# Deformable attention on one core: the first image's softmax beside the second image's position network

## The chip, the core and the metric

The kernel runs on one core of a Trainium2 chip. Its engines are named as in the profile: PE (TensorE, matmuls and transposes; PEld is its weight load), DVE (VectorE), ACT (ScalarE), POOL (GpSimd) and SP (SyncE, which here only issues DMAs). Each engine takes its instructions in order; they meet through semaphores. The metric is the device time of one execution in microseconds, lower is better. The kernel before takes 3842.15 us, the median of three runs (3840.60 to 3842.97).

## What is computed

Four layers run one after the other on x of 2 images x 512 channels x 32 x 32, all in float32. The change touches layer 0, an attention of 1024 queries over 64 sampled keys with 8 heads per image. To each score comes a bias: a small network with two hidden layers of 128, computed for each pair of query and key from their difference in position. Cut to what matters:

```python
bias = jnp.sign(pos) * jnp.log1p(jnp.abs(pos))
bias = relu(bias @ cpb_w1 + cpb_b1)
bias = relu(bias @ cpb_w2 + cpb_b2)
bias = (bias @ cpb_w3 + cpb_b3).reshape(b, GROUPS, H * W, Hd * Wd)
sim = jnp.einsum('bhid,bhjd->bhij', qh, kh) + bias
attn = jax.nn.softmax(sim, axis=-1)
out = jnp.einsum('bhij,bhjd->bhid', attn, vh)
out = jnp.einsum('bchw,oc->bohw', out, out_w) + out_b
x = x + out                                  # then an MLP of 2048 hidden channels
```

Layers 1 to 3 (a deformable convolution with gathers, a linear attention, a full attention) follow.

## The kernel before, in words

**Tiling.** A tile has 128 partitions and usually 1024 columns, the pixels of an image. Two heads share a tile, 64 keys each, so that the scores of both images are eight tiles: `simT[:, p, :]` with p = 0 to 3 for image 0 and p = 4 to 7 for image 1.

**The position network** (`biased_scores`) is one loop over p and j, where j goes over the 32 pairs of keys of a half: 8 x 16 = 128 steps. A step handles eight keys in four groups (t = 0 to 3), each of two keys:

- `hidden` (L868): DVE adds the two parts of the first layer into a tile h (128x1024). A relu follows, on DVE (L875) for three keys of sixteen and on ACT (L877) for the others. There are six h buffers, so that DVE can be at most three groups ahead of PE.
- `second_layer` (L888): PE multiplies the pair of h by w2 into two tiles `ph` of two PSUM banks each, 8 matmuls for each, four at a time in different columns of the array. ACT drains the first (`lo`, L898) and the second (`hi`, L900), and DVE adds them, weighted (L901). The pool `ps_h` has three buffers of ph. They take turns: the third ph after one needs its buffer again.
- `last_layer` (L909): PE sums the four `hi` of the step before over the 128 hidden units into `sim`, two further PSUM banks. It is issued after the second group of a step.
- At step j = 0 DVE stores the finished scores of the p before (`store`, L931). At j = 8 and j = 24, `first_layer` loads the next parts (`ab`) through SP and scales four tiles on ACT (L533).

**The softmax** (`Softmax`). `attention(p)` transposes the scores of one p on PE, eight transposes into one tile `pt` (L992), so that the keys lie along the columns; DVE takes the maximum of each run of 64 (L998) and subtracts it into `e` (L1000); ACT takes exp in place (L1001); DVE sums (L1003), inverts (L1004) and multiplies (L1005). `turn(p, e)` transposes back on PE into `pb` (L1012), and ACT copies it over the scores in simT (L1017). For image 0 this stands at the end of `biased_scores`, in the PSUM buffers of the network (`pt` and `pb` are tiles of `ps_h`, with the same tag as `ph`) and in its SBUF buffers. Image 1's softmax is done later, woven into the MLP of image 0, through `Softmax.image`.

**What follows.** `projected` multiplies the values by the output weights (`pm`, L1040, copied by ACT at L1041), `project` multiplies the attention of image 0 by that (`po`, L1052), and the MLP of image 0 begins (`ph`, L1112; `acc`, L1101). Its second weights `mlp_w2` (4 MB) are loaded through SP (L217) when the network's buffers come free.

**What sets the order.** PE runs in the order in which the code calls it (a manual schedule). DVE and ACT are ordered by the framework's scheduler, which may put an instruction that is ready ahead of one that stands earlier in the code. Semaphores and buffers' waits come from the framework. A pool's buffer is given again when its last reader is done.

Of the kernel before, what the change touches and what calls it, by code (L numbers as in the profile page):

```python
# [10 lines left out]
F32 = mybir.dt.float32  # L11
# [7 lines left out]
CC = 4  # L19
HW = 1024  # L20
# [230 lines left out]
def chain(*parts):  # L251
    for part in parts:
        yield from part
# [23 lines left out]
def layers(net, out):  # L277
# [12 lines left out]
    with ExitStack() as later:  # L290
# [12 lines left out]
        with ExitStack() as l0a:  # L303
            l0a.enter_context(net.tc.manual_schedule(engines={mybir.EngineType.PE}))

            q_flat = new_room()[:, : (NP * 36 + 6) * 34]
            q_pad = q_flat[:, : NP * 36 * 34].rearrange("p (n y x) -> p n y x", y=36, x=34)
            keys = net.pool(l0a, "l0_k")
            kbd = keys.tile([128, NP, 128], F32, name="kbd", tag="kbd")
            dram = net.pool(l0a, "cpb_dram", space=bass.MemoryType.DRAM)  # L310
            feat = dram.tile([32, 2048], F32, name="feat_d", tag="feat_d")
            w2 = keys.tile([128, 128], F32, name="w2_t", tag="w2")
            first = net.pool(l0a, "cpb_ab", 4)
            parts = queries_keys_values(net, bn, simT, q_flat, q_pad, kbd, val, feat, first)
            nc.sync.dma_start(out=w2, in_=net.ins["w2"])

            def load_weights():
                t = new_room()
                w1 = t[:, : 4 * 2048].rearrange("p (k m) -> p k m", m=2048)
                out_w = t[:, 4 * 2048 :].rearrange("p (k m) -> p k m", m=C)  # L320
                nc.sync.dma_start(out=out_w, in_=net.ins["out_w"])
                nc.sync.dma_start(out=w1, in_=net.ins["mlp_w1"])
                return w1, out_w

            w1, out_w = biased_scores(
                net, q_pad, kbd, feat, w2, simT, first, parts, load_weights
            )
# [499 lines left out]
def biased_scores(net, q_pad, kbd, feat, w2, simT, first, parts, load_weights):  # L827
# [12 lines left out]
    with ExitStack() as ctx:  # L840
        small = net.pool(ctx, "cpb_w", 1)
        hid1 = net.pool(ctx, "cpb_h1", 6)
        lows = net.pool(ctx, "cpb_lo", 2)
        highs = net.pool(ctx, "cpb_hi", 6)
        ps_h = net.psum(ctx, "cpb_ps_h", 3)
# [6 lines left out]
        size = small.tile([128, 1], F32, name="size", tag="size")  # L852
# [51 lines left out]
        def last_layer(sim, j, sums):  # L904


            for n in range(2):
                for t in range(4):
                    nc.tensor.matmul(  # L909
                        sim[32 * t : 32 * t + 32, half(n)],  # L910
                        lhsT=w3[:, 30 - j : 62 - j],
                        rhs=sums[t][:, half(n)],
                        start=(j == 0),
                        stop=(j == 30),
                        skip_group_check=True,
                    )
# [13 lines left out]
        def store(p, sim):  # L930
            nc.vector.tensor_scalar(simT[:, p, :], sim, net.vec("cpb_b3"), None, ALU.add)  # L931

        pending = None
        sim = None
        hidden_done = 0
        for p, j in [(p, j) for p in range(NP) for j in range(0, 32, 2)]:
# [20 lines left out]
                if p == NP - 1:  # L957
                    weights = load_weights()
            pending = (p, j, sums)


        def two_banks(name):
            return ps_h.tile([128, HW], F32, name=name, tag="ph")

        def one(name, size):
            if size == HW:
                pool, tag = (hid1, "h1") if name == "e" else (highs, "hi")
                return pool.tile([128, HW], F32, name=name, tag=tag)
            return small.tile([128, size], F32, name=name, tag=f"soft_{name}", bufs=2)

        soft = Softmax(net, simT, one, two_banks)
        es = [soft.attention(p) for p in range(2)]
        last_layer(sim, *pending[1:])
        es += [soft.attention(p) for p in range(2, CC)]
        for p, e in enumerate(es):
            soft.turn(p, e)
        store(NP - 1, sim)
        return weights

# [1 line left out]
class Softmax:  # L981
# [4 lines left out]
        self.net, self.simT, self.one, self.banks = net, simT, one, banks  # L986

    def attention(self, p):
        nc, one = self.net.nc, self.one
        pt = self.banks("pt").rearrange("p (h j) -> p h j", j=64)  # L990
        for c in range(8):
            nc.tensor.transpose(  # L992
                pt[:, 2 * c : 2 * c + 2, :].rearrange("p h j -> p (h j)"),
                self.simT[:, p, 128 * c : 128 * c + 128],
                self.net.cst("ident"),
            )
        m = one("m", 16)
        nc.vector.tensor_reduce(m, pt, AX.X, ALU.max)  # L998
        e = one("e", HW).rearrange("p (h j) -> p h j", j=64)
        nc.vector.tensor_tensor(e, pt, m.unsqueeze(2).to_broadcast([128, 16, 64]), ALU.subtract)  # L1000
        nc.scalar.activation(e, e, AF.Exp)  # L1001
        s = one("s", 16)
        nc.vector.tensor_reduce(s, e, AX.X, ALU.add)  # L1003
        nc.vector.reciprocal(s, s)  # L1004
        nc.vector.tensor_tensor(e, e, s.unsqueeze(2).to_broadcast([128, 16, 64]), ALU.mult)  # L1005
        return e

    def turn(self, p, e):

# [1139 lines left out]
```

## Time and profile before

| | us |
|---|---|
| median of three runs (lowest, highest) | 3842.15 (3840.60, 3842.97) |
| the profiled execution | 3841.13 |
| its span, from the first to the last instruction | 3839.4 |
| mean granted TensorE clock | 0.990 |

By stretches of the span (a program sums each engine's busy time between two times):

| stretch, us | what runs | PE | DVE | ACT |
|---|---|---|---|---|
| 0 to 88 | queries, keys, values, sampling | 64.1 | 58.3 | 63.2 |
| 88 to 2104 | position network, both images | 2004.0 | 1914.7 | 1955.5 |
| 2104 to 2135 | softmax of image 0, start of the projection | 19.0 | 21.3 | 12.4 |
| 2135 to 2430 | projections, softmax of image 1, MLP of image 0 | 295.0 | 53.4 | 48.1 |
| 2430 to 3839 | MLP of image 1, layers 1 to 3 | 1352.6 | 717.4 | 487.6 |

The page gives busy times and, for the idle time of an engine, what ended it (the releaser). A row of the timeline has its start, its duration, engine, line, operation, what it writes and reads, how many instructions are merged into it (xN), and in brackets the idle time before it with its releaser. A float32 matmul shows as two records, one for each of its two passes. The duration of one instruction includes its start and its end, which lie beside the neighbours; in a row of work without gaps, an instruction costs the time from its start to the next one's start, which is less.

### The profile page before, as it was taken

The page shows a single profiled execution, that of the slowest core. Times are in us where ns is not written, and L with a number is a line of the kernel's source. Part 1 is how long each engine was busy: PE and PEld are TensorE (multiplying, and loading weights), DVE is VectorE, ACT ScalarE, POOL GpSimd, SP SyncE. Part 2 cuts the span into 40 slices and gives each one's busy share as a digit, 9 for nine tenths or more (in the row PEclk, how much of TensorE's full clock was granted, in tenths as well). Part 3 has the DMA queues.
Part 4 walks back from the last instruction along what each step waited for, and adds up shares of the span by engine and source line. Part 5 has one row for each costly group of instructions (what it writes and reads, how often), then busy time and mean ns, then how long its engine had stood idle before and what let it go on. Part 6 is the DMA issues. An engine that isn't in the chain of part 4 may idle for free. (4 is left out here: it accounts for less than half of the span.)

```text
span 3839.4 us, 59395 instructions
## 1 busy us (share of the span) xinstructions
PE 3734.6 (97%) x25356; PEld 1492.3 (39%) x25356; DVE 2765.1 (72%) x3242; ACT 2566.8 (67%) x2941; POOL 188.2 (5%) x180
## 2 busy tenths in 40 slices
PE   7999999999999999999999899999979999899999
PEld 4532222223222322232233444444434544455555
DVE  6999999999999999999999310510475482566565
ACT  7999999999999999999999211211123243345544
POOL 0000000000000000000000000000252150000000
PEclk9999999999999999999999999999989999999999
DMA  3000000000000000000010000022455471000000
GB/s 111 1 23 23 23 1 23 23 23 12 12 23 23 21 3 23 23 23 1 23 56 29 33 0 1 18 82 77 134 173 187 144 273 48 1 12 1 1 20 25
DMA packets 54459, 168.57 MB, mean 44 GB/s; under 512 B 4804, under 2 KB 10436, under 8 KB 51252
## 3 DMA queue, kind: packets, MB, share of 16 engines
q1 hardware_dynamic: 31556, 83.77, 6.3%
q0 software_dynamic: 21776, 79.14, 6.2%
q8 instruction: 200, 3.28, 0.4%
q10 hardware_dynamic: 864, 1.86, 0.1%
q14 instruction: 63, 0.52, 0.0%
HBM read 156.11 MB, written 8.65 MB: 43 GB/s over the span
## 5 line engine op out<-in xcount | busy, mean ns | idle before, releaser
L888 PE MATMUL ph<-h,w_t 128*32 128x512 f32 x16384 | 1796.8, 593 | 14.0 <-ACT lo L898 6.5
L868 DVE TENSOR_TENSOR h<-ab 128x1024 f32<-128x1024 f32 x1024 | 1206.0, 1219 | 73.2 <-PE ph L888 72.2
L888 PEld LDWEIGHTS ph<-h,w_t 128*32 128x32 f32 x16384 | 548.7, 110 | 1235.5 <-issue 1031.2
L877 ACT ACTIVATE h<-h 128x1024 f32<-128x1024 f32 x832 | 869.6, 1065 | 44.4 <-DVE h L868 40.6
L901 DVE SCALAR_TENSOR_TENSOR hi<-lo,low_w,hi 128x1024 f32<-128x1024 f32 x512 | 655.0, 1279 | 27.4 <-ACT hi L900 26.8
L900 ACT ACTIVATE hi<-ph,size_b,size 128x1024 f32<-128x1024 f32 x512 | 620.5, 1212 | 15.5 <-PE ph L888 10.1
L898 ACT ACTIVATE lo<-ph,vec_t 128x1024 f32<-128x1024 f32 x512 | 571.1, 1116 | 3.8 <-PE ph L888 3.8
L2071 ACT ACTIVATE e<-pl,m 128x1024 f32<-128x1024 f32 x128 | 143.6, 1122 | 228.1 <-DVE m L2063 228.1
L1552 PE MATMUL po<-fold,turned 128*128 128x512 f32 x576 | 269.7, 612 | 3.1 <-DVE dfacc L1560 2.9
L2063 DVE TENSOR_REDUCE m<-pl 128x1 f32<-128x1024 f32 x128 | 150.8, 1220 | 144.4 <-PE pl L1973 144.4
L1120 ACT ACTIVATE h<-ph,vec_t 128x512 f32<-128x512 f32 x64 | 44.0, 687 | 310.9 <-PE ph L1112 310.4
L909 PE MATMUL sim<-hi,w 128*32 128x512 f32 x2048 | 246.1, 592 | 0.6 <-DVE hi L901 0.6
L1112 PE MATMUL ph<-xn,room 128*128 128x512 f32 x512 | 230.2, 593 | 0.0
L1101 PE MATMUL acc<-h,mlp_w_t 128*128 128x512 f32 x512 | 229.8, 592 | 0.0
L1499 DVE SCALAR_TENSOR_TENSOR sum<-got,wts,sum 128x256 f32<-128x256 f32 x432 | 184.4, 479 | 48.1 <-ACT sum L1495 45.7
L1475 POOL DMA_INDIRECT got<-table,idx x144 | 174.0, 1209 | 550.4 <-DVE sum L1499 272.1
L2025 PE MATMUL pt<-cst_t,e 128*128 128x128 f32 x1024 | 148.2, 278 | 6.5 <-ACT aT L2036 3.9
L2025 PEld LDWEIGHTS pt<-cst_t,e 128*128 128x128 f32 x1024 | 117.9, 141 | 93.2 <-issue 61.0
L1552 PEld LDWEIGHTS po<-fold,turned 128*128 128x128 f32 x576 | 107.8, 197 | 114.8 <-issue 109.7
L1101 PEld LDWEIGHTS acc<-h,mlp_w_t 128*128 128x128 f32 x512 | 97.3, 190 | 122.5 <-issue 122.0
L1112 PEld LDWEIGHTS ph<-xn,room 128*128 128x128 f32 x512 | 96.2, 190 | 117.2 <-issue 116.6
L1526 ACT COPY turned<-pt 128x512 f32<-128x512 f32 x72 | 41.9, 582 | 145.9 <-PE pt L1520 145.7
(250 smaller groups left out, 2712.1 us busy)
## 6 DMA issues: line engine op xcount, KB each, us to landing
ab<-feat_d SPq DMA_DIRECT2D x64, 512.0 KB, 3.8
room<-in_dc_w_dram SPq DMA_DIRECT2D x9, 1024.0 KB, 4.7
dc_w_t<-in_dc_w_dram SPq DMA_DIRECT2D x5, 1024.0 KB, 4.8
room<-in_mlp_w_dram SPq DMA_DIRECT2D x1, 4096.0 KB
mlp_w_t<-in_mlp_w_dram SPq DMA_DIRECT2D x1, 4096.0 KB, 13.4
dc_w_t<-in_dc_w_dram SPq DMA_DIRECT2D x8, 512.0 KB, 5.1
w_qkv_t<-in_w_qkv_dram SPq DMA_DIRECT2D x3, 1024.0 KB, 8.9
out_dram<-x_all SPq DMA_DIRECT2D x12, 256.0 KB, 2.0
```

The source lines that it names most:

```text
L868: nc.vector.tensor_tensor(h1.rearrange("p (y x) -> p y x", x=32), at_x[:, k : k + 1, :].to_broadcast([128, 32, 32]), at_y[:, k, :].unsquee ...
L877: nc.scalar.activation(h1, h1, AF.Relu)
L888: nc.tensor.matmul(ph[32 * t : 32 * t + 32, half(n)], lhsT=w2[:, c0 : c0 + 32], rhs=pair[t // 2][:, half(n)], start=True, stop=True, skip_ ...
L898: nc.scalar.activation(lo, phs[0], AF.Relu, bias=b2_lo)
L900: nc.scalar.activation(hi, phs[1], AF.Relu, bias=size_b, scale=size)
L901: nc.vector.scalar_tensor_tensor(hi, lo, low_w, hi, ALU.mult, ALU.add)
L909: nc.tensor.matmul(sim[32 * t : 32 * t + 32, half(n)], lhsT=w3[:, 30 - j : 62 - j], rhs=sums[t][:, half(n)], start=(j == 0), stop=(j == 30 ...
L1101: nc.tensor.matmul(accs[oc], lhsT=self.w2[:, m, 128 * oc : 128 * oc + 128], rhs=hs[m], start=(m == 0), stop=(m == 15),)
L1112: nc.tensor.matmul(ph, lhsT=self.w1[:, k, 128 * m : 128 * m + 128], rhs=xn[:, k, :], start=(k == 0), stop=(k == CC - 1),)
L1499: nc.vector.scalar_tensor_tensor(t[:, q, :], g[:, s, :], w, t[:, q, :], ALU.mult, ALU.add)
L1552: nc.tensor.matmul(self.out, lhsT=turned[:, at : at + 128], rhs=self.folded.w[k][:, i, :], start=(k == 0 and i == 0), stop=(k == 8 and i = ...
L2025: nc.tensor.transpose(pt[:, 128 * c : 128 * c + 128], e[:, 128 * k : 128 * k + 128], ident)
```

## The change

The softmax of image 0 is cut into steps and moved into the loop of the position network, to where it works on image 1 (p from 4 to 7). `Softmax.attention` becomes a generator, `parts`, that yields after the subtraction, after the sum and after the multiplication; `steps` runs through them and then through `turn`. The loop takes one step at every fourth j (j = 4, 12, 20 and 28), sixteen steps in all for the four tiles of image 0. The small tiles and `e` get a pool of their own with one buffer of each (`cpb_e`), while `pt` and `pb` stay tiles of the ring of three `ph` buffers. `attention` runs through all parts as before, for image 1. Behind the loop only the last `last_layer` and `store` are left.

```diff
@@ biased_scores
+        exps = net.pool(ctx, "cpb_e", 1)
+
+        def two_banks(name):
+            return ps_h.tile([128, HW], F32, name=name, tag="ph")
+
+        def one(name, size):
+            return exps.tile([128, size], F32, name=name, tag=f"soft_{name}")
+
+        soft = Softmax(net, simT, one, two_banks)
+        beside = chain(*(soft.steps(p) for p in range(CC)))
+
         pending = None
         sim = None
         hidden_done = 0
...
             pending = (p, j, sums)
-
-
-        def two_banks(name):
-            return ps_h.tile([128, HW], F32, name=name, tag="ph")
-
-        def one(name, size):
-            if size == HW:
-                pool, tag = (hid1, "h1") if name == "e" else (highs, "hi")
-                return pool.tile([128, HW], F32, name=name, tag=tag)
-            return small.tile([128, size], F32, name=name, tag=f"soft_{name}", bufs=2)
-
-        soft = Softmax(net, simT, one, two_banks)
-        es = [soft.attention(p) for p in range(2)]
+            if p >= CC and j % 8 == 4:
+                next(beside, None)
+        for _ in beside:
+            pass
         last_layer(sim, *pending[1:])
-        es += [soft.attention(p) for p in range(2, CC)]
-        for p, e in enumerate(es):
-            soft.turn(p, e)
         store(NP - 1, sim)
         return weights

@@ class Softmax
     def attention(self, p):
+        parts = self.parts(p)
+        for e in parts:
+            pass
+        return e
+
+    def steps(self, p):
+        for e in self.parts(p):
+            yield
+        self.turn(p, e)
+        yield
+
+    def parts(self, p):
         nc, one = self.net.nc, self.one
...
         nc.vector.tensor_tensor(e, pt, m.unsqueeze(2).to_broadcast([128, 16, 64]), ALU.subtract)
+        yield e
         nc.scalar.activation(e, e, AF.Exp)
         s = one("s", 16)
         nc.vector.tensor_reduce(s, e, AX.X, ALU.add)
+        yield e
         nc.vector.reciprocal(s, s)
         nc.vector.tensor_tensor(e, e, s.unsqueeze(2).to_broadcast([128, 16, 64]), ALU.mult)
-        return e
+        yield e
```

## The prediction

> **What bounds the kernel now.** I read the page first, then the stage's busy time by windows, then the waits, then the timeline where the stage ends. The page's chain of waits is of no use here: its earliest piece lies at 2781 us, after everything that the change touches. The page's slices show where to look: between 88 and 2104 us (the position network of both images) all three big engines are nearly full, and just behind lies a hole. The windows, one over a whole pass p of 16 steps (247 us) and three over the end of the stage:
>
> ```profile
> core 0: us, PE busy (x) PEld busy (x) DVE busy (x) ACT busy (x) POOL busy (x), PEclk, DMA share, GB/s
> 1572.00:1819.00 247.00, 245.48 (x2272) 72.80 (x2264) 234.68 (x213) 240.80 (x236) 0.00 (x0) 1.00 0.06 18
> 2112.00:2120.00 8.00, 1.72 (x11) 1.55 (x12) 8.00 (x10) 3.12 (x3) 0.00 (x0) 0.76 0.41 174
> 2120.00:2128.00 8.00, 4.54 (x22) 3.80 (x21) 6.46 (x8) 2.98 (x3) 0.00 (x0) 0.50 0.00 0
> 2136.00:2164.00 28.00, 28.00 (x66) 12.19 (x65) 8.20 (x12) 0.41 (x1) 0.00 (x0) 1.00 0.00 0
> ```
>
> In a pass PE is idle for 1.5 of 247 us: it is the bound, one step each 15.45 us. DVE is idle for about 12 us and ACT for 6. From 2112 us it is the other way round: DVE is full, PE works little, and its granted clock falls to 0.76 and 0.50. The timeline of PE over that hole:
>
> ```profile
> 2104.05 1.97 PE L992 MATMUL pt<-cst_t,simT 128*128 128x128 f32 x16
> 2105.95 1.06 PE L909 MATMUL sim<-hi,w 128*32 128x512 f32 x6
> ...
> 2114.72 1.06 PE L1012 MATMUL pb<-cst_t,e 128*128 128x128 f32 x8 [3.27 <-DVE e L1005]
> 2119.34 1.94 PE L1012 MATMUL pb<-cst_t,e 128*128 128x128 f32 x8 [3.56 <-DVE e L1005]
> 2124.00 1.94 PE L1012 MATMUL pb<-cst_t,e 128*128 128x128 f32 x8 [2.72 <-DVE e L1005]
> 2126.68 1.94 PE L1012 MATMUL pb<-cst_t,e 128*128 128x128 f32 x8 [0.74 <-DVE e L1005]
> 2129.72 5.51 PE L1040 MATMUL pm<-room,val 128*128 128x512 f32 x8 [1.10 <-ACT simT L1017]
> 2135.06 1.45 PE L1052 MATMUL po<-simT,outv 128*128 128x512 f32 x3
> ```
>
> The last matmul of the network starts before 2104.05; the first of the next full stretch (L1052) at 2135.06. These **31.0 us** are image 0's softmax, 20 passes of DVE over 128x1024 in a row with PE behind them.
>
> **What the change removes.** Compared engine by engine, the two built programs issue the same instructions; only the softmax of image 0 has moved, and a few DVE and ACT instructions around it swap places. With T for 2104.05 (the network's last matmul done), what is left at the end of the stage:
> - The last ACT drain of ph (L900, 2104.19 to 2105.40) and the last DVE sum (L901, 1.28, now with nothing before it) end at T+2.7.
> - The two pm matmuls that stand before the last L909 need the bank that this ACT drain frees (in the trace pm waits in the same way for the last copy of pb, 0.06 us after its end): they start at T+1.4. A 128x512 matmul takes two passes of 0.43 (27.6 us for the 64 passes of L1052), so they end at T+3.1. The remaining five L909 take some 1.7 (16 passes take 1.9), to T+4.8; the other two pm 1.7, to T+6.5. The ACT copies (0.59 each) run beside it; po waits for the first of them only.
> - So po starts at T+6.5 instead of T+31.0: **24.5 us** off. The clock stays up too, since no PE gap of 3 us is left.
>
> What is late next? The 4 MB of mlp_w2 are issued at 2104.2 and take 13.4 us; their first reader, L1101, starts at 2173, 69 us later, and would still be 44 us behind. The softmax issues no DMA, and the SP and POOL queues keep their order; POOL's pad memset, which waited for the last pb, is read hundreds of us later. After the stage everything keeps its order and only moves earlier.
>
> **What it adds on PE.** Eight transposes in and eight back for each p, into a stretch where PE has no room, so at full price. The nearest row is the same transposes of image 1 between hot matmuls:
>
> ```profile
> 2176.60 1.04 PE L992 MATMUL pt<-cst_t,simT 128*128 128x128 f32 x8
> 2177.47 3.60 PE L1112 MATMUL ph<-xn,room 128*128 128x512 f32 x8
> ```
>
> From start to start eight cost 0.87 us. Sixteen for four p: 4 x 1.74 = **7.0 us**.
>
> **What it adds on DVE and ACT.** Per p on DVE: maximum, subtraction, sum, multiplication at 1.14 from start to start, reciprocal 0.24: 4.8 us, against 12 idle. On ACT: exp and copy, 2.1 us, against 6 idle. So both fit on average, and the cost is only what PE waits while they catch up. The order in which the built program issues says where this is: maximum and subtraction stand in DVE's queue behind one L868 and around one L901, the sum nine instructions later, the normalisation fifteen after that. The steps, written four loop steps (62 us) apart, thus come within some 35 us as far as DVE is concerned. The place for the first p, seen in the timeline of before:
>
> ```profile
> 1137.80 13.92 PE L888 MATMUL ph<-h,w_t 128*32 128x512 f32 x128
> ...
> 1143.73 1.28 DVE L901 SCALAR_TENSOR_TENSOR hi<-lo,low_w,hi 128x1024 f32<-128x1024 f32 x1
> 1144.92 2.35 DVE L868 TENSOR_TENSOR h<-ab 128x1024 f32<-128x1024 f32 x2
> ```
>
> The group before pt ends at 1144.67; pt runs to 1145.6. DVE does one L868 from 1144.92, the maximum from 1146.1, one L901, the subtraction from 1148.4 to 1149.5. pt takes one of three ph buffers, and the third ph after pt needs it again. By then PE has written two others (1.72 each), to 1149.0: it waits **0.5 us**. Queued behind these on DVE are two L868 and a relu (L875) for a group that PE starts at 1153.2; they were done by 1149.6 and will be by about 1152. After the sum, DVE is 3.5 us behind less what it makes up (0.7 us a step), so a relu on DVE can be late by some tenths.
>
> A burst of the same kind is in the trace: twice a pass, ACT scales four ab tiles (L533, 1.22 each, 4.2 us from start to start), beside a DVE store (L931, 1.28) in the first burst. PE's only gaps beside the first burst of the pass p = 4:
>
> ```profile
> 1100.88 3.64 PE L888 MATMUL ph<-h,w_t 128*32 128x512 f32 x32 [0.30 <-ACT hi L900]
> ...
> 1111.85 8.96 PE L888 MATMUL ph<-h,w_t 128*32 128x512 f32 x80 [0.47 <-ACT lo L898]
> ```
>
> That is 0.77 us for 5.4 us of added work, 0.14 per us; the softmax's 6.9 us would cost 1.0 by that. I take **1.0 us per p, 4.0 in all**. Bounds: 0 (all absorbed) and 6.9 per p (nothing absorbed); near the low one, because the burst row is of the same engines and the same queue.
>
> **Two rules against it.** (1) The burst row prices a busy engine, not a lent bank. The Trainium skill, "Perfetto Trace Analysis", section Optimizing Tensor Performance (Matmuls), wants matmul groups to rotate through different PSUM banks, so that draining one lies beside the next. Here a third of the rotation is lent eight times to something drained by DVE. If each loan stopped PE for its whole drain (2.3 for pt, 1.0 for pb), it would be 4 x 3.3 = 13.2 instead of 4.0, and the gain 4.3. No run here has shown such a loan; the walk above gives 0.5, because two other buffers keep PE fed for 3.4 us. (2) The first exp brings its table load into the full stage: 1.28 us by the row at 2105.41. "ScalarE: Activation LUTs", What ACT_TABLE_LOAD costs, adds a drain, 2.66 in all. It is one load (the built order has no other in this stage, and before had one too); at 0.14 per us it is 0.2 or 0.4. I leave it in the range.
>
> **The sum.** -24.5 + 7.0 + 4.0 = -13.5 us. The profiled execution took 3841.13 with a span of 3839.4; it becomes 3827.6. The median of the runs shown, 3842.15, lies 1.0 above it: **3829 us**. What this kernel's measurement can tell from no change is about 0.2%, 7.7 us.
>
> **Rivals.**
> - *Nothing stalls*: PE pays only its transposes, -17.5: 3825. For it: DVE's 12 idle us a pass. Against: the gap of 0.5 at pt. Chance 0.08.
> - *The lent bank costs most of its drain* (rule 1), or the end of the stage keeps some 6 us through waits on the last sums: -4 to -7, 3835 to 3838. For it: DVE's order puts an L901 between maximum and subtraction, and that L901 waits for ACT. Against: the walk. Chance 0.19.
> - *DVE and ACT become the bound*, the slower side: an in-order DVE that has lost its lead hands PE each relu late, and PE frees h buffers late, so that the idle time that DVE had in waiting for PE is not there to catch up with. All 6.9 us appear: 4 x (1.74 + 6.9) = 34.6, less 24.5, is +10: 3852. It decides from 6.1 us per p, that is 4.4 of stall. For it: DVE at 95% and ACT at 97% of the pass. Against: the bursts recover within a step or two. Chance 0.10.
> - *It doesn't do what it says* (softmax left at the end): excluded by the built order.
>
> The forecast itself, 3823 to 3834: 0.63. Faster by over 0.2%: 0.63 + 0.08 = 0.71; within: 0.19; slower: 0.10. Range 3821 to 3840: it takes in the forecast, no stalls, and most of the middle rival.
>
> **What would show it.** Right: L1052's first matmul some 13 us earlier than 2135, about 6.5 us after the last L888; PE gaps of about 1 us per p from 1144 on, on waits for ACT or DVE, first at the third ph after pt; the granted clock 1.00 from 2104 on. Wrong: PE gaps of over 4 us per p, or a step that stays longer than 15.45 us well past the last pb; or a po that waits for something else than the last pm.

## The result, and the profile after

The changed kernel takes **3836.49 us** (median of 20 runs) against 3842.85 for the kernel before on the same chip (20 runs, 3839.74 to 3846.77). The ratio, taken without one disturbed run of 7279.8 us, is 0.9979, with a 95% interval of 0.9973 to 0.9985: about 8 us faster (the medians lie 6.4 apart). A ratio of 1 lies outside the interval, but the gain is hardly larger than the 0.2% that the forecast gave as the bound of what can be told. The profiled execution took 3837.59 us, with a span of 3835.8.

So the forecast (3829) had the sign and the range right, and the gain too large: -13 forecast, -8 measured. The stretches of the two profiles show where. "Stage" is the time from the first L909 burst to the last L888's end (T), "tail" from there to the first matmul of `po`:

| us | before | after | forecast | measured |
|---|---|---|---|---|
| stage | 1992.53 | 2007.01 | +7.0 +4.0 | +14.5 |
| tail | 31.0 | 7.8 | -24.5 | -23.2 |
| both | 2023.54 | 2014.83 | -13.5 | **-8.7** |

The rest of the program took 1711.1 us in this profile and 1704.3 in the one of before, so the two profiled spans differ by only 3.5; the rest is taken up under the kernel before, profiled again.

The windows over the pass p = 6 (from one L909 burst to the burst 16 steps on), before and then after, and of after over the tail and the start of the projection:

```profile
core 0: us, PE busy (x) PEld busy (x) DVE busy (x) ACT busy (x) POOL busy (x), PEclk, DMA share, GB/s
1624.91:1877.04 252.13, 250.61 (x2316) 74.36 (x2312) 239.76 (x218) 245.46 (x241) 0.00 (x0) 1.00 0.05 18
1630.78:1886.38 255.60, 253.93 (x2332) 75.98 (x2328) 244.59 (x223) 247.44 (x243) 0.00 (x0) 1.00 0.05 18
2116.86:2124.68 7.82, 6.67 (x29) 1.88 (x22) 2.57 (x2) 2.87 (x4) 2.02 (x1) 1.00 0.87 335
2124.68:2140.00 15.32, 15.32 (x37) 6.92 (x37) 4.09 (x6) 0.59 (x1) 0.00 (x0) 1.00 0.32 137
```

DVE has gained 4.83 us of work and ACT 1.98, as forecast (4.8 and 2.1), and the pass is 3.47 us longer. In the tail PE now works for 6.67 of 7.82 us at a granted clock of 1.00, where it was 0.76 and 0.50. The timeline of after over the tail (PE, and the one row of ACT that PE waits for):

```profile
2116.86 1.03 PE L909 MATMUL sim<-hi,w 128*32 128x512 f32 x6
2118.36 1.98 PE L1055 MATMUL pm<-room,val 128*128 128x512 f32 x4 [0.48 <-ACT hi L900]
2120.28 1.90 PE L909 MATMUL sim<-hi,w 128*32 128x512 f32 x10
2122.22 1.07 ACT L1056 COPY outv<-pm 128x512 f32<-128x512 f32 x2 [3.91 <-PE sim L909]
2122.86 1.98 PE L1055 MATMUL pm<-room,val 128*128 128x512 f32 x4 [0.68 <-ACT outv L1056]
2124.68 1.53 PE L1067 MATMUL po<-simT,outv 128*128 128x512 f32 x3
```

The order is the one forecast (L909, pm, L909, pm, po). What was missed is in the fourth row: ACT did not copy the first two pm when they were done at 2120.3, but stood idle for 3.91 us until the last L909 had ended. The trace's records show why: no matmul of these two pm updates PE's semaphore, and the next update stands on the last L909, so that nothing told ACT earlier. The second pair of pm needs those copies and starts 0.68 us late. With the first pm 0.1 later than forecast, and the three pieces up to `po` counted at 1.7 each instead of 1.8 to 1.9, that makes T+7.8 instead of T+6.5.

The rest of the loss is in the stage. The windows of four steps of the pass p = 5, before:

```profile
1388.22:1403.67 15.45, 15.45 (x149) 4.68 (x144) 15.16 (x15) 15.02 (x16) 0.00 (x0) 1.00 0.00 1
1403.67:1419.12 15.45, 15.45 (x149) 4.68 (x144) 14.56 (x14) 14.72 (x15) 0.00 (x0) 1.00 0.01 2
1419.12:1434.57 15.45, 15.45 (x149) 4.68 (x144) 15.17 (x15) 15.02 (x16) 0.00 (x0) 1.00 0.00 1
1434.57:1450.02 15.45, 15.45 (x149) 4.68 (x144) 14.56 (x14) 14.72 (x15) 0.00 (x0) 1.00 0.00 1
```

And the same steps after:

```profile
1390.64:1407.26 16.62, 16.62 (x157) 5.42 (x153) 16.34 (x15) 15.91 (x17) 0.00 (x0) 1.00 0.01 2
1407.26:1423.07 15.81, 15.65 (x147) 4.53 (x142) 15.81 (x16) 14.84 (x15) 0.00 (x0) 1.00 0.01 1
1423.07:1438.95 15.88, 15.88 (x152) 4.97 (x148) 15.85 (x16) 14.05 (x14) 0.00 (x0) 1.00 0.00 1
1438.95:1454.86 15.91, 15.91 (x151) 4.77 (x147) 15.79 (x15) 15.62 (x16) 0.00 (x0) 1.00 0.00 1
```

The first of each four is the step with the transposes: +1.16. The three behind it are 0.36, 0.43 and 0.46 longer, and in them DVE is busy for 15.81 of 15.81, 15.85 of 15.88 and 15.79 of 15.91 us. A step on DVE before left 0.3 to 0.9 us free; subtraction, sum and normalisation, which the scheduler puts within two steps of each other, are more than that. For three steps DVE, not PE, sets the time.

Only a part of this appears as idle time of PE. The windows over the whole stage, of after and then of the kernel that has nothing of image 0's softmax but the transposes (below):

```profile
109.85:2116.86 2007.01, 1995.23 (x18361) 619.32 (x18354) 1911.44 (x1734) 1942.95 (x1900) 0.00 (x0) 1.00 0.06 19
109.62:2109.24 1999.62, 1990.78 (x18361) 618.96 (x18354) 1893.09 (x1714) 1936.13 (x1891) 0.00 (x0) 1.00 0.06 19
```

After is 7.4 us longer with the same 18361 records on PE. Of these, 4.5 count as busy and 2.9 as idle (11.8 against 8.8). The timeline of after in the second of those steps shows how a wait hides in busy time (rows of PEld, PE and one of DVE; PEld's are weight loads, one for each matmul of a pass, and normally four come every 0.43 us):

```profile
1418.41 0.13 PEld L888 LDWEIGHTS ph<-h,w_t 128*32 128x32 f32 x4 [0.30 <-issue]
1418.84 0.12 PEld L888 LDWEIGHTS ph<-h,w_t 128*32 128x32 f32 x2 [0.30 <-issue]
1419.27 0.12 PEld L888 LDWEIGHTS ph<-h,w_t 128*32 128x32 f32 x2 [0.31 <-issue]
1419.71 0.69 DVE L875 TENSOR_SCALAR h<-h 128x1024 f32<-128x1024 f32 x1
1420.45 0.16 PEld L888 LDWEIGHTS ph<-h,w_t 128*32 128x32 f32 x8 [1.06 <-DVE h L875]
1420.46 3.20 PE L888 MATMUL ph<-h,w_t 128*32 128x512 f32 x26 [0.16 <-DVE h L875]
```

The relu of the group's second key runs from 1419.71 to 1420.40. Until then only the two column groups of the first key can run: two slots of 0.43 us with two matmuls in place of four. Then come those that had to wait. PE looks busy throughout (its own row shows 0.16 us of idle time); the loss is in the half-filled slots.

### The profile page after: what moved, and what is told of

Read it like the earlier page. It is cut to its first block, busy times and chain, and to the rows that moved or that the text cites. A ratio compares the mean times of both kernels' runs of the same rounds, so it can differ in the third digit from the quotient of the medians.

```text
span 3835.8 us, 59384 instructions
## 1 busy us (share of the span) xinstructions
PE 3739.0 (97%) x25356; PEld 1487.3 (39%) x25356; DVE 2765.5 (72%) x3242; ACT 2566.4 (67%) x2941; POOL 189.1 (5%) x180
## 5 line engine op out<-in xcount | busy, mean ns | idle before, releaser
L888 PE MATMUL ph<-h,w_t 128*32 128x512 f32 x16384 | 1808.0, 593 | 15.7 <-ACT lo L898 6.5
L888 PEld LDWEIGHTS ph<-h,w_t 128*32 128x32 f32 x16384 | 547.6, 110 | 1239.9 <-issue 1017.2
L901 DVE SCALAR_TENSOR_TENSOR hi<-lo,low_w,hi 128x1024 f32<-128x1024 f32 x512 | 654.8, 1279 | 31.6 <-ACT hi L900 30.3
L909 PE MATMUL sim<-hi,w 128*32 128x512 f32 x2048 | 251.0, 592 | 0.0
```

The lines of the kernel that those rows point to most:

```text
L888: nc.tensor.matmul(ph[32 * t : 32 * t + 32, half(n)], lhsT=w2[:, c0 : c0 + 32], rhs=pair[t // 2][:, half(n)], start=True, stop=True, skip_ ...
L901: nc.vector.scalar_tensor_tensor(hi, lo, low_w, hi, ALU.mult, ALU.add)
L909: nc.tensor.matmul(sim[32 * t : 32 * t + 32, half(n)], lhsT=w3[:, 30 - j : 62 - j], rhs=sums[t][:, half(n)], start=(j == 0), stop=(j == 30 ...
```

## The experiments

The numbers of the stage and of stage plus tail come from one profile each. In the kernels of the experiments, lines behind an edit stand a few numbers lower down.

**The changed kernel once more**, with no edit:

> The changed kernel once more, to see what of its profile comes back. In the first profile the stretch from the first sum (L909) to the last L888 of the position network took 2007.0 us against 1992.5 before, and the rest from the last L888 to L1067's first matmul 7.8 against 31.0: together 8.7 us less. But from there to the end of the span it took 1711.1 us against 1704.3 before, with the same instructions in the same order. Theory 'jitter': the stage comes back within 0.3 us (2007.0 and 7.8), the rest does not and lies anywhere between 1702 and 1713; time 3834 +- 4 and a ratio to before of 0.9978 (8.7 us). Rival 'given back later': the change shifts the gathers against each other, and the rest is again 1709 to 1713.

3835.39 us (11 runs), ratio 0.998 (0.9971 to 0.9989). Stage 2007.02, tail 7.8: within 0.02 us of the first profile, step by step. So differences of tenths in the stage can be read. The rest took 1709.5 us, which fits both of the expectations and so decides nothing between them.

**The sum and the normalisation held to their written steps.** They may not start before an L901 of the step in which the code calls them:

```diff
-            nc.vector.scalar_tensor_tensor(hi, lo, low_w, hi, ALU.mult, ALU.add)
+            added.append(nc.vector.scalar_tensor_tensor(hi, lo, low_w, hi, ALU.mult, ALU.add))
...
-                next(beside, None)
+                if j in (12, 20):
+                    with net.tc.issue_after(added[-3].ins):
+                        next(beside, None)
+                else:
+                    next(beside, None)
```

> The sum and the normalisation on DVE are held back to the loop steps in which the code asks for them (62 us apart), instead of 9 and 24 instructions behind the subtraction; nothing else moves. Theory 'late h' (DVE loses its lead, h tiles reach PE late in the three steps after pt): the extra 0.36 to 1.0, 0.43 and 0.46 us of these steps go, 5.7 us over four p; the stage takes 2001 to 2002 us, and the time falls by 5 to 6 us against the changed kernel. Rival 'lent bank' (PE waits since pt holds one of three ph buffers): nothing changes, 2007 us, same time.

3829.5 us (6 runs), ratio 0.9967 (0.9955 to 0.9979); stage 2003.16. The three late steps are gone (15.45 us; 15.58 for the one with the table load). The gain on the changed kernel is 3.85 us of the stage, not the 5 to 6 expected: the sum now falls ahead of the ab burst. Windows of this kernel, a step behind the transposes and the step of the burst; then the step of the burst before; then a row of ACT from this kernel, behind the sum (DVE, 1456.77):

```profile
1421.47:1436.92 15.45, 15.45 (x148) 4.68 (x144) 15.44 (x16) 15.04 (x16) 0.00 (x0) 1.00 0.01 1
1467.83:1484.72 16.89, 16.27 (x149) 4.27 (x145) 15.21 (x15) 16.89 (x18) 0.00 (x0) 1.00 0.20 63
```
```profile
1465.47:1481.63 16.16, 15.86 (x149) 4.41 (x145) 14.48 (x14) 16.16 (x17) 0.00 (x0) 1.00 0.19 66
```
```profile
1459.75 1.06 ACT L877 ACTIVATE h<-h 128x1024 f32<-128x1024 f32 x1 [0.74 <-DVE h L868]
```

In the burst's step ACT is the full engine: 16.89 of 16.89 us, with 18 instructions. Before it had 17 there, in 16.16. ACT had stood idle for 0.74 us behind the sum, waiting for an h, and so came into the step in which it has no room one instruction late.

**pt copied out of its bank at once**, so that the loan of the ph buffer ends with one ACT copy and does not wait for DVE's two passes:

```diff
+        if copied:
+            nc.scalar.copy(e, pt)
+            pt = e
         nc.vector.tensor_reduce(m, pt, AX.X, ALU.max)
```

> For image 0, ACT copies pt out of PSUM at once, and DVE takes maximum and subtraction from SBUF; the lent buffer comes back after one ACT copy (1.0 us) instead of three DVE instructions (3.5 us). Rival 'lent bank': the stage shortens by 3 us or more, to below 2004. Theory 'late h': no gain; the additional ACT copy (1.0 us a p, beside 6 us of idle time) costs 0 to 2 us in all: 2007 to 2009.

3832.16 us (8 runs), ratio 0.9972 (0.9962 to 0.9983); stage 2006.66. The step with pt is 16.61 us here, in the changed kernel and with everything but the transposes left out (below). The loan costs nothing that can be seen. The lateness has only come together in one step, where DVE is again the full engine (16.74 of 16.77):

```profile
1390.59:1407.20 16.61, 16.61 (x156) 5.43 (x152) 16.32 (x16) 15.96 (x17) 0.00 (x0) 1.00 0.01 2
1422.65:1439.42 16.77, 16.08 (x149) 4.37 (x145) 16.74 (x17) 14.66 (x16) 0.00 (x0) 1.00 0.00 1
```

**Only the transposes.** Of image 0's softmax the transposes of simT into pt and into pb are kept, at their places; the rest of it is left out:

```diff
-        for e in self.parts(p):
+        for name in ("pt", "", "", "pb"):
+            if name:
+                out = self.banks(name)
+                for c in range(8):
+                    cols = slice(128 * c, 128 * c + 128)
+                    self.net.nc.tensor.transpose(
+                        out[:, cols], self.simT[:, p, cols], self.net.cst("ident")
+                    )
             yield
-        self.turn(p, e)
-        yield
```

> Of image 0's softmax only the sixteen PE transposes of each p are left, in the same places, of scores into pt and pb, which nothing reads; maximum, subtraction, exp, sum, normalisation and the copy back are left out. It prices the transposes alone. The prediction had 0.87 us for eight, 7.0 in all: the stage would take 1999.5 us. By the first profile of the changed kernel eight take 1.0 to 1.16: 8.2 to 9.3, 2000.7 to 2001.8. Both theories: no extra time in the steps after pt (15.45 each). The rest to L1067 stays at 7.8.

3824.82 us (4 runs), ratio 0.9957 (0.9942 to 0.9972); stage 1999.62, that is +7.1 us on before. Windows of it, the step of the transposes back and the step of the ab burst behind it:

```profile
1577.89:1594.50 16.61, 16.61 (x156) 5.42 (x152) 15.71 (x15) 16.57 (x17) 0.00 (x0) 1.00 0.19 64
1594.50:1609.95 15.45, 15.45 (x148) 4.61 (x144) 13.43 (x13) 15.45 (x17) 0.00 (x0) 1.00 0.21 70
```

Eight transposes lengthen a step by 1.16 us, not 0.87. But the burst's step takes 15.45 instead of 16.16: the likely reading is that ACT gets ahead while PE transposes, so that PE's gap in that step closes. Three passes have such a step: 8 x 1.16 - 3 x 0.71 = 7.15. What DVE and ACT add to PE's time in the changed kernel is therefore 2007.01 - 1999.62 = **7.4 us**, where the forecast had 4.0.

**The sum further from the burst** (key pair 10 instead of 12, held):

```diff
-            if p >= CC and j % 8 == 4:
-                if j in (12, 20):
+            if p >= CC and j in (4, 10, 20, 28):
+                if j in (10, 20):
```

> Both later steps are held to their written places, and the sum's step stands at key pair 10 instead of 12, so that it no longer runs beside the ab burst of VectorE. Theory (what is left of the lateness is a collision with that burst, 0.74 us three times): the step after the ab burst is back at 16.16 us instead of 16.9, and the stage from the first L909 burst to the last L888 takes 2003.2 - 2.2 = 2001.0 us; the time falls by some 2 us against the version with the sum at 12 (3829.5), to 3827 or 3828. Rival (the sum costs its own time on VectorE wherever it stands, 0.7 us): another step grows by 0.7 and the stage stays at 2003.2.

3830.95 us (7 runs), ratio 0.9968 (0.9957 to 0.9979); stage 2001.29. The burst's step is 16.15 again in two passes (16.43 in the first), so the collision was the cause. (The ab burst is ACT's, not VectorE's as the expectation says.) In the total this gain of 1.9 us cannot be seen.

**The whole softmax later, the transposes just ahead of the burst** (pt at key pair 12, sum at 18, normalisation at 22):

```diff
-            if p >= CC and j in (4, 10, 20, 28):
-                if j in (10, 20):
+            if p >= CC and j in (12, 18, 22, 28):
+                if j in (18, 22):
```

> The whole softmax of one channel chunk is moved later: transposes at key pair 12, just ahead of the step that the ab burst stretches from 15.45 to 16.16 us; sum at 18, normalisation at 22, both held to their places; transposes back at 28 as before. Theory (such a gap of TensorE's takes up 0.71 of what the transposes cost, as it does behind the transposes back): the step of the transposes is 16.61, the one behind it 15.45 instead of 16.16, and the stage takes 2001.0 - 4 x 0.71 = 1998.2 us. Rival (the subtraction of 1.1 us on VectorE, which must follow pt at once, meets the ab burst and costs what the sum cost there, 0.7 us or more): the step behind stays at 16.16 or above and the stage is at 2001 to 2004 us.

3827.28 us (5 runs), ratio 0.996 (0.9947 to 0.9974); stage 2000.01, between the two expectations. Windows of it, the step with the transposes and the two behind:

```profile
1452.00:1469.32 17.32, 16.82 (x157) 5.31 (x152) 16.84 (x16) 17.26 (x18) 0.00 (x0) 1.00 0.18 62
1469.32:1484.77 15.45, 15.45 (x149) 4.68 (x144) 15.32 (x15) 15.29 (x16) 0.00 (x0) 1.00 0.20 69
1484.77:1502.23 17.46, 17.46 (x157) 5.14 (x152) 15.79 (x15) 17.42 (x18) 0.00 (x0) 1.00 0.01 2
```

Before, these were 15.45, 16.16 and 18.13. The gap of 0.71 was not filled: it has moved into the step of the transposes, which ACT now stretches. But the step after is 0.67 shorter, so that the transposes in cost 0.49 instead of 1.16 in the passes p = 5 and 6. In p = 4 these three steps take 1.56 more than before, and in p = 7, which has no ab burst, 1.16.

**Only the normalisation held**:

```diff
-                if j in (12, 20):
+                if j == 20:
```

> Of the change only the normalisation is held to its written place (key pair 20); the sum may still run early, one step behind the subtraction. If the normalisation makes the two late steps behind it by itself (0.43 and 0.46 us for each chunk), these are gone, the step of the sum keeps its 0.36 us (1.01 for the first chunk), and the stage takes 2007.0 - 3.6 = 2003.4 us. If the lateness is a queue that starts with the sum and only drains through the next steps, the steps behind it still show 0.2 us or more each and the stage stays above 2004.5 us.

3833.35 us (10 runs), ratio 0.9977 (0.9968 to 0.9986); stage 2005.74, and neither expectation is met as a whole. The two late steps behind the normalisation are gone and the one behind the sum stays (15.81), as the first theory says. But of the 0.88 us saved a pass, 0.55 comes back four steps later, in the burst's step (16.83 against 16.29), where no instruction of the softmax stands:

```profile
1471.08:1487.91 16.83, 16.54 (x153) 5.23 (x149) 14.89 (x15) 16.83 (x18) 0.00 (x0) 1.00 0.19 63
```

Again ACT has 18 instructions there in place of 17. This reads as a lead that DVE and ACT lose to the early sum, that is carried from step to step without PE losing any time, and that is charged where ACT is full; in the changed kernel the three slow steps would have let them catch up.

**The kernel before, profiled again**:

> The kernel before, profiled once more. The stage from the first L909 burst to the last L888 should take 1992.5 us again, within 0.1, and the stretch from there to the first matmul of the gather stage 31.0 us; the rest, 1704.3 us in the first profile and 1704.2 to 1711.1 in those of the changed kernels, which run the same instructions there in the same order. If that rest is another number within these bounds, its spread is that of the gathers from one execution to the next; if it is 1704.3 again within 0.3, the spread over the changed kernels is left to explain.

3841.68 us in one run. Stage 1992.44, tail 31.9 (31.0 in the first profile), both together 2024.33. The rest of the program takes 1705.1, where the first profile had 1704.3. Over the profiles of the changed kernels it lies between 1703.7 and 1711.1, in no order that follows the edits. So the rest is not constant within some 7 us; what sets it was not tried, and two profiles of before do not show whether the change has a part in it.

**pb copied by VectorE**, in the last two schedules:

```diff
-        self.turn(p, e)
+        self.turn(p, e, self.net.nc.vector.tensor_copy)
...
-        self.net.nc.scalar.copy(self.simT[:, p, :], pb)
+        (copy or self.net.nc.scalar.copy)(self.simT[:, p, :], pb)
```

In the one with pt at key pair 4:

> The version with the sum at key pair 10 (transposes at 4), and the same copy of pb on VectorE. Theory: the step behind the transposes back is 15.45 instead of 15.90, and the stage takes 2001.3 - 1.4 = 1999.9 us, 0.3 us above the version that has nothing but the transposes (1999.6): VectorE's four other operations then cost nothing. Rival: the stage stays at 2001.3 us or above.

3827.56 us (6 runs), ratio 0.996 (0.9948 to 0.9973); stage 1999.86 (expected 1999.9). The step behind the transposes back, in the version with the copy on ACT and then in this one:

```profile
1596.22:1612.12 15.90, 15.65 (x148) 4.52 (x144) 13.98 (x14) 15.90 (x17) 0.00 (x0) 1.00 0.21 68
```
```profile
1595.77:1611.22 15.45, 15.45 (x148) 4.65 (x144) 13.76 (x13) 15.45 (x17) 0.00 (x0) 1.00 0.19 70
```

In the one with pt ahead of the burst:

> The version with the transposes ahead of the ab burst (pt at key pair 12, sum at 18, normalisation at 22), and in it the copy of pb into simT on VectorE instead of ScalarE. ScalarE is the full engine of the step behind the transposes back (15.91 of 15.91 us busy, VectorE 13.98). Theory (the copy's lateness on ScalarE is what keeps that step at 15.91 instead of 15.45): the step is 15.45, the stage takes 2000.0 - 3 x 0.46 = 1998.6 us and the time falls another 1.4 us, to some 3826. Rival (the copy of 1.2 us on VectorE makes the step of the transposes back or its follower late instead, VectorE being busy for 15.81 of 16.61 us there): the step of the transposes back or the next but one grows by 0.5 us or more and the stage stays at 2000 us or above.

**3825.82 us** (5 runs), ratio 0.9953 (0.994 to 0.9967); stage 1998.58 (expected 1998.6). It is the shortest stage with the whole softmax in it: about 18 us faster than before, where the change gives 8. The last two versions' medians cannot be told apart.

The totals bear the stage out: against before's two profiles (2023.54 and 2024.33 for stage and tail, mean 2023.9) this last version saves 17.5 us in those stretches and some 18 by its ratio; the one with only transposes 16.5 and 16.5, the first held version 13.0 and 12.7, the changed kernel 9.1 and 8.1. In the other six the two numbers lie 0.7 to 2.5 us apart, within the intervals of the ratios.

## Why the forecast was right, and where its sizes were wrong

The account was right in its parts: the tail goes, PE pays the transposes, and DVE and ACT make PE wait for some us. The total was inside the stated range partly by luck. The median of 3836.5 lies above the forecast's own band (3823 to 3834) and in that of the lent bank (3835 to 3838), whose mechanism the runs refute.

**The tail was right, 1.3 us short.** The forecast took 24.5 us off; the profile shows 23.2 (24.1 against the second profile of before). The term that failed is "the ACT copies run beside it": they began only after the last L909, which is 0.7 of the 1.3; the rest is 0.1 to 0.2 in each piece. The granted clock stays at 1.00, as forecast.

**The transposes were right by luck, through two errors.** 7.0 forecast, 7.1 measured. The row of image 1's transposes, 0.87 for eight, was not near enough: among the network's matmuls eight cost 1.16, 9.3 in all. What gives 2.1 back is the gap of the ab burst, which the forecast had as a row of its own but did not count as cover.

**The stalls are the term that was mis-sized: 4.0 forecast, 7.4 measured.** By steps: 4 x 1.25 behind subtraction, sum and normalisation; 0.65 more for the first pass, which has the table load (its step behind pt is 16.46, the others' 15.81); 3 x 0.46 for the copy of pb on ACT; 3 x 0.13 at the burst. The stall was real and came from the lead that DVE loses, as the forecast had it, but the sign that it named first, a PE gap at the third ph after pt, did not come. Three things in its working were wrong.

- *The 0.5 us at pt do not exist.* "The third ph after pt needs it again" was taken from the order of the code. In the timeline of after, the 64 records of L888 behind pt are four tiles of 1.7 us each. The third begins at 1403.8, while the subtraction, last reader of pt, ends only at 1404.2. So the third tile has another buffer than pt's: one that was released earlier, and not the next in turn. The fourth begins at about 1405.5, when pt's buffer is free, and no row shows a wait:

```profile
1399.34 1.09 PE L1005 MATMUL pt<-cst_t,simT 128*128 128x128 f32 x8
1400.36 7.07 PE L888 MATMUL ph<-h,w_t 128*32 128x512 f32 x64
1402.95 1.22 DVE L1013 TENSOR_TENSOR e<-pt,m 128x1024 f32<-128x1024 f32 x1
1407.26 1.90 PE L909 MATMUL sim<-hi,w 128*32 128x512 f32 x16
```

- *The row of the ab burst was read by PE's idle time alone.* That gave 0.77 us, or 0.14 per us of added work. The windows of before over the two steps of such a burst, here at the start of the pass p = 6:

```profile
1592.46:1608.62 16.16, 15.86 (x149) 4.41 (x145) 14.47 (x14) 16.16 (x17) 0.00 (x0) 1.00 0.20 66
1608.62:1624.91 16.29, 15.83 (x149) 4.43 (x145) 16.05 (x16) 16.25 (x17) 0.00 (x0) 1.00 0.00 1
```

  PE is idle for 0.30 and 0.46 us, but the steps are 0.71 and 0.84 longer than 15.45, with the same 149 records. By the length of its steps the burst cost 1.55 us, 0.29 per us, and the softmax's 6.9 us a p would have come to 2.0, or 7.9 in all. That this is near 7.4 may be chance, since the burst loads ACT, while the softmax loads DVE three times in a row.
- *The room was counted by the pass, not by the step.* (The prediction's window of 247 us is also less than a pass, which takes 252.13; the 12 us of idle time on DVE hold.) 4.8 us on DVE do fit into 12 idle, as the last version with pt at key pair 4 shows: 1999.86 against 1999.62 with none of them. They do not fit into the few steps into which the scheduler draws them, with 0.3 to 0.9 us free in each.

**The rules weighed.** The Trainium skill's rule to rotate matmul groups through PSUM banks ("Perfetto Trace Analysis", Optimizing Tensor Performance (Matmuls)) gives no price; the prediction's reading of it, that each loan stops PE for its whole drain, would have made 13.2 us. A loan of one buffer in three cost 0.00 here, since the step with pt is 16.61 whether DVE, ACT or nothing drains it. The table load shows as 1.28 us in the trace of after, at 1149.09, and no drain shows beside it: ACT's instruction before ends at 1149.08, and the exp starts at 1150.38. The first pass alone has this load, and its step is 0.65 longer than the others'. When DVE has room, 0.13 is left in that step and 0.27 in the first pass's step of the burst. No run took the load away, so that it is the cause is argued.

**The rivals.** "DVE and ACT become the bound" named the mechanism, an in-order DVE without its lead that hands over each relu late. It holds in three steps of a pass, not in all, so 7.4 us came out of its 27.6. The lent bank is refuted. "Nothing stalls" is what the spread version with pb copied by VectorE reaches to 0.2 us.

## What to carry to other kernels

When work is moved beside a stage that is nearly full, count each engine's free time by the step in which the scheduler really puts the work, not over the whole stage, and hold it there if it drifts together; here the softmax's instructions on DVE and ACT cost 7.4 us bunched, 1.7 spread, and 0.2 spread with one copy moved from ACT to DVE. Look also for the step where another engine is already the full one: lateness that costs nothing on its way is charged there, so keep added work clear of it or put it on the engine that has room. A ring of buffers need not be refilled in turn: here a tile took a buffer that was free earlier, so what comes late next is not read from the order of the code. And an engine that needs a result starts when a semaphore tells it, here with the next matmuls' end, 1.9 us after the result was there.

## What was not expected of the hardware

- **A wait that looks like work.** With one of two inputs late, PE ran two of its four column groups alone, two matmuls per 0.43 us slot instead of four. Of the 7.4 us of stalls, 4.5 stand in PE's busy time and 2.9 in its idle time. In this kernel the length of a step shows a stall in full, the list of waits does not.
- **The same transposes at two prices**: eight in 0.87 us between full-width matmuls, and 1.16 between the ones that use 32 columns each. In the trace 0.2 of the difference lies where the one kind follows the other: the first transpose starts 0.54 us after the last slot of L888, whose slots are 0.43 apart, and L888 starts 0.20 after the last transpose, where transposes are 0.11 apart. Why was not tried.
- **Idle time can be cover for PE's own added work**: 1.16 us of transposes ahead of a step that ACT stretches gave 0.67 to 0.71 back in the steps behind.
